# Image 1's first MLP product in two groups of fifteen on quarters

## The chip, the cores and the metric

The kernel runs on one core of a Trainium2 chip. The metric is the device time of one execution in microseconds, the median of several runs. A core has five engines with a queue of instructions each: PE multiplies matrices, DVE and ACT work element by element, POOL and SP issue most of the transfers. Each takes its instructions in the order written and waits at semaphores for the others.

## The reference

Eight images of 384 channels and 32 x 32 points, all in 32 bit, go through two layers.

```python
# layer 0, per image; tokens are the 1024 points
x1  = x + proj(attention(layernorm(x)))
h   = gelu(layernorm(x1) @ w_fc1.T + b_fc1)      # 384 -> 1536
y   = x1 + h @ w_fc2.T + b_fc2                   # 1536 -> 384
# layer 1, per image
z   = layernorm(depthwise_conv_7x7(y))
z   = gelu(z @ w1 + b1)                          # 384 -> 1536
z   = gamma * z * nx(z) + gbeta + z              # nx: a norm over the image
out = y + z @ w2 + b2                            # 1536 -> 384
```

## The kernel before

**Tiles.** Channels lie on the 128 partitions: an image is three tiles of 128 x 1024, the hidden layer twelve. Most work goes by halves of 512 points (`half`), and a matrix product of 128 x 128 by 128 x 512 is the unit; one such product is two passes in the trace.

**Products by thirds.** A 3 x 3 by 3 x 2 product of blocks takes 18 block products done directly. `tiles_by_thirds` (L458) does it in fifteen, in the order `SINGLY` (L94): each product takes a sum of weight blocks, made once and kept in DRAM, and a sum of data blocks, and `SUMS` says which results are added (DVE L483 and L486, ACT L480 and L488). The ten sums of data blocks are made on DVE, by `make_thirds` (L441) or, on 256 points, by `make_quarters` (L447, line L455).

**One round.** For image b the order of work is: qk by thirds, attention (L807), proj, fc1, fc2 (`by_thirds`, L1049, fifteen forms of four products, p0 to p14), and then for image b-1 the second layer: `grn_up` (h, w1) and `grn_down` (w2). The 7 x 7 convolution of image b-1 runs meanwhile, tap by tap on DVE (L1244: one multiply-add over an image's channel tile, 841 to 961 elements per partition), with some taps done by ACT and POOL (L1279, L1280). For image 0's convolution `start_conv` is called at L2115 and runs beside image 1's qk, attention and fc1. Images 2 to 7 find five taps of two channel tiles done already (`begin_convolution`); image 0's convolution has no such start.

**Who sets the order.** The program is written out by hand through `Flow` (L137). PE code calls `flow.pe(us)`, which moves a planned clock forward; chains (generators) that are due by that clock then write their next instructions, on DVE, ACT, POOL or SP, into the program. So a chain's `yield 1.5` is a planned distance and not a measured one, and once written the order on each engine is fixed. `flow.finish(chain)` writes the rest of a chain at once. While the list `hold` is not empty, `convolution` writes no tap (L1222) and `freely` (L1535) keeps the chains behind it back.

**fc1 (mlp, L1004).** For images 2 to 6 `fast_fc1` (L227) is true. Then the first half's tiles 6 to 11 are done by `gelu_group` (L952) in two groups of fifteen products on quarters: group 0 before tile 0, group 1 after tile 5; tiles 0 to 5 and the whole second half are direct (`gelu_half`, three products each, line L415). `hold` is set during group 0 and again from `rest()`, which is called after tile 1, to the end of group 1. `rest()` finishes attention's second half and does its proj (L760, L768). Then the second layernorm's second half is spawned (L551, L554, L561, L568, L572, L575, L594; its sums over channels on PE are L518, or L532 when the halves of the partitions are first folded by a POOL transfer, L526); with the groups its last three steps wait at the gate `ln2`. For images 0, 1 and 7 all twelve tiles are direct, `rest()` comes after tile 3, and nothing is held.

**The second layernorm's first half** runs under attention's second half, spawned in `attention` with `slow` and `wait`, which stretch its planned distances: 1.35 and 5.2 for image 1, 1.0 and 4.5 for the others but the last. For images with the groups, `make_quarters` follows in the same chain.

**What follows the second half's layernorm.** `conv_norm` (L1929) hangs two chains on it: `norm_of_next` (L1975), image 2's first layernorm, with the adds L2007 and L2009, POOL folds L1984 and L1991, and the PE sums L2001; and `end_soon` (L1971), which finishes the convolution, that is, writes all taps that are left in one go, then waits 22 planned us for image 1 (11 later on), and goes on with layernorm 3 of the convolution's result (again L551, L554, fold L526, PE sum L532, L561).

**Weights.** A ring of nine tiles is filled by SP in a fixed plan (L1888, `plan_fc1` L356). With the groups an image's fc1 takes twelve tiles, six of them sums from DRAM, in place of six.

Of the kernel before, what the change touches and what calls it, by code (L numbers as in the profile page):

```python
# [52 lines left out]
B, C, H, W = 8, 384, 32, 32  # L53
# [123 lines left out]
def block_kernel(  # L177
# [41 lines left out]
    exact = [False]  # L219
# [5 lines left out]
    s_fc1 = dram.tile([P, 2, len(FORMS), P], F32, tag="s_fc1", bufs=1, name="s_fc1")  # L225

    def fast_fc1(b):  # L227
        return not exact[0] and 1 < b < B - 1

    def half(h):  # L230
        return slice(h * NH, (h + 1) * NH)
# [16 lines left out]
    eps0 = const.tile([P, 1], F32, name="eps0")  # L248
# [558 lines left out]
    def attention(b, xt, qT, kT, last_tile, ready, first, next_image):  # L807


        sums = two.tile([P, 2 * NP * 8], F32, tag="sums", name=f"sums_{b}")  # L810
        outs, chains, ps, backs = {}, {}, {}, ({}, {})

        def scores(qh, m, t):
            s = ps_s.tile([P, 2, NH], F32, tag="s", name=f"s_{b}_{qh}_{m}_{t}")
            for j in range(2):
                for i in range(2):
                    k0 = t * P + 64 * i
                    nc.tensor.matmul(  # L818
                        out=s[64 * i : 64 * i + 64, j, :],
                        lhsT=kT[64 * j : 64 * j + HD, m, k0 : k0 + 64],  # L820
                        rhs=qT[64 * j : 64 * j + HD, m, half(qh)],
                        start=True,
                        stop=True,
                    )
            flow.pe(U)
            p = three.tile([P, 2, NH], F32, tag="p", name=f"p_{b}_{qh}_{m}_{t}")
            nc.scalar.activation(p, s, AF.Exp)  # L827
            return p

        def product(qh, m, t, p):  # L830
            if t == 0:
                for i in range(2):
                    outs[i] = o_tile(f"o_{b}_{qh}_{m}_{i}")
            for i in range(2):
                keys = slice(64 * i, 64 * i + 64)
                for j in range(2):
                    at = (2 * m + j) * VW
                    nc.tensor.matmul(  # L838
                        out=outs[i][64 * j : 64 * j + 64, :],
                        lhsT=v[keys, t, at : at + 64],  # L840
                        rhs=p[keys, j, :],
                        start=(t == 0),
                        stop=(t == KT - 1),
                    )
            flow.pe(U)
            if t == KT - 1:
                chains[qh, m] = flow.spawn(average(b, qh, m, dict(outs), sums, backs[qh]))

        steps = [(qh, m, t) for qh in range(2) for m in ORDER for t in range(KT)]
        ln_table()  # L850
        ln = None
        for n in range(len(steps) + 2):
            if n == 1:
                hold.clear()
                quiet.clear()
            if n == 2:
                last_tile()
            if n < len(steps):
                if steps[n][0] == 0 and steps[n][2] == 0:
                    ready(steps[n][1])  # L860
                ps[n] = scores(*steps[n])
            if n >= 2:
                product(*steps[n - 2], ps.pop(n - 2))
            if n - 2 in (len(steps) // 2 - 9, len(steps) - 9):
                quiet.append("averages")
            if n - 2 == len(steps) // 2 + 6:
                for chain in first:
                    flow.finish(chain)
                xn = one.tile([P, CT, N], F32, tag="xn", bufs=2, name=f"xn2_{b}")
                for m in (NP - 1, *range(CT)):  # L870
                    flow.finish(chains[0, m])
                proj(b, xt, 0)
                quiet.clear()
                next_image(b)
                slow = {1: 1.35, B - 1: 1.2}.get(b, 1.0)
                fold = "columns" if b else None
                ln = layernorm(xt, xn, 0, eps0, "g2", f"ln2_{b}", False, spaced=True, slow=slow, fold=fold, wait=5.2 if b == 1 else 4.5)
                if fast_fc1(b):
                    ln = sequence(ln, make_quarters(xn, hidden(b), 1.5))
                ln = flow.spawn(ln)  # L880

        def rest():
            for m in (NP - 1, *range(CT)):
                flow.finish(chains[1, m])
            for seen, op in ((low, ALU.min), (high, ALU.max)):
                ext = small.tile([P, 1], F32, tag="ext", name=f"ext_{b}_{op.name}")
                nc.vector.tensor_reduce(ext, sums, AX.X, op)
                nc.vector.tensor_tensor(seen, seen, ext, op)
            proj(b, xt, 1)
            quiet.clear()  # L890

        return ln, rest, xn
# [974 lines left out]
    def main():  # L1867
# [5 lines left out]
        xn = load_x(0, "xn", 4)  # L1873
# [13 lines left out]
        xt = load_x(0, "x", engine=nc.gpsimd)  # L1887
# [198 lines left out]
        for b in range(B):  # L2086
            if b == 0:
                folding = flow.spawn(after(None, folds(weights), 8))
                preparing = flow.spawn(after(None, prepare(weights, False), 4))
                singly = [flow.spawn(after(None, sums_for_tiles(i), 33 + 5 * i)) for i in range(2)]  # L2090
                aside = flow.spawn(after(folding, prepare(weights, True), 4))
            if b:
                flow.finish(state["thirds"])
            q_and_k = qk(b, state["xn"], weights if b else None)
            ln2, rest, xn = attention(b, xt, *q_and_k, (folding, aside) if b == 0 else (), next_image)
            if b == 0:
                for chain in singly:
                    flow.finish(chain)
                fc1_sums = flow.spawn(after(None, sums_for_fc1(), 22.0))
                shift = flow.spawn(after(None, prepare(weights, None), 4.0))  # L2100
            if b < B - 1:
                mlp(b, xt, xn, weights, b, ln2, rest, lambda: before_fc2(b), lambda ln: conv_norm(b, ln))
            else:
                acc = state["acc"]
                mlp_by_halves(b, xt, xn, weights, ln2, rest, last_convolution)
                fine = whether_fine()
            kept[b] = keep(b, xt)
            if b + 1 < B:
                acc = state["acc"]
            if b == 0:  # L2110
                xt = load_x(b + 1, "x")
                flow.finish(preparing)
                flow.finish(fc1_sums)
                flow.finish(shift)
                start_conv(b, 1.6, (9, 1.65), (10, 22.0), (60, 1.5))  # L2115
                next_values(1)
                continue
            if b < B - 1:
                xt = load_kept(b - 1, kept.pop(b - 1))
            flow.finish(state["norm3"])  # L2120
            if b < B - 1:
                flow.finish(state["w1"])
                y, gx = grn_up(b - 1, weights, b - 1, lambda: begin_conv(b))
                flow.finish(state["begin"])
                start_conv(b, 1.65 if b == B - 2 else 1.85, (23, 2.4), (24, 9.0), (25, 26.0), (72, 1.5))
                scale = flow.spawn(grn_scale(b - 1, gx, weights, b - 1, y))
                next_values(b + 1)
                flow.finish(scale)
                quiet.append("w2")
                grn_down(b - 1, y, xt, weights, b - 1, b - 1)  # L2130
                quiet.clear()
                xt = load_x(b + 1, "x")
            else:

                norm_b = flow.spawn(after(state["conv"], last_norm(LAST[1], 0.85)))
                norm_c = flow.spawn(after(norm_b, last_norm(LAST[2], 1.2)))
                y, gx = grn_up_straight(b - 1, acc, weights, b - 1)
                scale = flow.spawn(grn_scale(b - 1, gx, weights, b - 1))
                flow.finish(state["norm_a"])
                sums = small.tile([P, CT + 1, HT], F32, tag="gx_last", bufs=1, name="gx_last")  # L2140
                y_last = places(y)
                last_up(last[0], y_last, 0, sums, weights)
                flow.finish(scale)
                halves = lambda k, part: y[:, k, part]
                blocks = [(r, half(n)) for r in range(CT) for n in range(2)]
                args = b - 1, halves, kept[b - 1], weights
                grn_down_straight(*args, b - 1, b - 1, blocks[:-1])
# [157 lines left out]
```

## Time and profile before

| | us |
|---|---|
| median of three runs | 3212.09 |
| lowest and highest of them | 3211.55, 3214.67 |
| the profiled execution | 3213.02 |
| its span, first to last instruction | 3211.1 |
| PE's mean granted clock | 0.999 |

The stages of images 1 and 2 in the profiled execution, in us from the span's start, where the first instruction of each begins on PE:

| | image 1 | image 2 |
|---|---|---|
| attention, second half | 442.6 | 834.9 |
| fc1, first product | 484.9 | 877.3 |
| proj, second half | 495.3 | 889.2 |
| fc2, p0 | 558.5 | 949.0 |
| grn_up | 612.8 | 1002.6 |

In a view by time a row gives the start, the length, the engine, the line, the operation, what is written and read, the shape and the count; in brackets stands the time the engine was idle before it and what ended that. In a view by stretches a row gives the stretch and its length, then for PE, PE's weight loads, DVE, ACT and POOL the busy time and the number of instructions, then PE's granted clock, the share in which the transfer engines worked, and GB/s.

### The profile page before, as it was taken

Reading aid. Unit: us, or ns where it says so; the run is one execution under the profiler, and the core shown is the slowest. Engines: PE = TensorE matmul, PEld = TensorE weight load, DVE = VectorE, ACT = ScalarE, POOL = GpSimd, SP = SyncE. Lnnn points to the kernel's source line nnn. Section 1 sums busy time; section 2 is a strip of 40 time slices with the busy share of each in tenths; the row PEclk is TensorE's granted clock in tenths of the full one; section 3 lists DMA queues with packets and bytes.
Section 4 is the critical chain, followed back from the end, with each engine's and each line's share of the span. In section 5 each row is a group of like instructions: output and inputs, shape, how many; then the busy total and the mean of one; then the engine's idle time right before and its main releaser. Section 6 shows DMA issues by size and latency. Waiting matters only on the chain.

```text
span 3211.1 us, 39348 instructions
## 1 busy us (share of the span) xinstructions
PE 3196.2 (100%) x14204; PEld 1402.1 (44%) x14204; DVE 2550.4 (79%) x3587; ACT 1674.6 (52%) x2363; POOL 493.4 (15%) x592
## 2 busy tenths in 40 slices
PE   9999999999999999999999999999999999999999
PEld 5344434443444434444344443444435444344454
DVE  4547788897878978789787888888887788879964
ACT  3542763456644476444754637637365374732543
POOL 2102211112111121201112011120111201200000
PEclk9999999999999999999999999999999999999999
DMA  6435742647346564456546374463743638433244
GB/s 210 155 127 170 168 90 50 162 112 165 84 88 159 123 151 92 97 142 158 115 92 124 116 186 97 81 136 106 194 92 80 148 97 200 72 81 93 55 119 111
DMA packets 206052, 393.09 MB, mean 122 GB/s; under 512 B 42656, under 2 KB 48416, under 8 KB 205472
## 3 DMA queue, kind: packets, MB, share of 16 engines
q0 software_dynamic: 79296, 163.35, 26.6%
q1 hardware_dynamic: 126272, 226.49, 23.6%
q8 instruction: 114, 1.87, 0.2%
q10 hardware_dynamic: 288, 0.71, 0.1%
q14 instruction: 82, 0.67, 0.1%
HBM read 212.98 MB, written 40.11 MB: 79 GB/s over the span
## 4 chain that ended last, share of the span: by engine, by line
PE 97%; DVE 1%; DMA 1%; ACT 0%; issue 0%; SPq 0%; DVEq 0%; ACTq 0%
PE fc L415 15%; PE s L818 13%; PE o L838 13%; PE o_p L496 11%; PE fc_p L496 11%; PE v L738 4%; PE proj L760 4%; PE h_n L467 3%; PE h_z L467 3%; PE h_x L467 3%; PE h_last L1427 2%; PE o L1378 2%; PE h L402 2%; PE qk_n L467 2%; PE qk_z L467 2%; PE qk_x L467 1%
## 5 line engine op out<-in xcount | busy, mean ns | idle before, releaser
L1244 DVE SCALAR_TENSOR_TENSOR acc<-pad,vec,acc 128x870 f32<-128x870 f32 (+8 forms) x815 | 911.0, 1157 | 2.7
L827 ACT ACTIVATE p<-s 128x1024 f32<-128x1024 f32 x512 | 524.3, 1025 | 255.2 <-PE s L818 246.9
L818 PE MATMUL s<-qk 48*64 48x512 f32 x4096 | 538.7, 591 | 0.4 <-ACT qk L660 0.2
L838 PE MATMUL o<-p,v 64*64 64x512 f32 x4096 | 535.7, 589 | 0.0
L1280 POOL DMA_DIRECT2D acc<-tap x266 | 227.0, 859 | 1354.9 <-ACT tap L1279 647.5
L415 PE MATMUL fc<-xn,fc 128*128 128x512 f32 x972 | 427.7, 594 | 0.1
L496 PE MATMUL o_p<-y,w 128*128 128x512 f32 x664 | 289.0, 592 | 0.0
L838 PEld LDWEIGHTS o<-p,v 64*64 64x64 f32 x4096 | 166.4, 132 | 273.3 <-issue 265.0
L415 PEld LDWEIGHTS fc<-xn,fc 128*128 128x128 f32 x972 | 183.1, 190 | 229.2 <-issue 220.5
L818 PEld LDWEIGHTS s<-qk 48*64 48x64 f32 x4096 | 162.3, 132 | 275.9 <-issue 213.1
L496 PE MATMUL fc_p<-qk,fc 128*128 128x512 f32 x520 | 226.6, 593 | 0.3 <-DMA qk<-qk 0.3
L1279 ACT ACTIVATE tap<-pad,vec 128x512 f32<-128x512 f32 x266 | 195.1, 736 | 2.9 <-DMA acc<-tap 2.9
L496 PEld LDWEIGHTS o_p<-y,w 128*128 128x128 f32 x664 | 125.6, 190 | 157.7 <-issue 146.4
L1244 DVE SCALAR_TENSOR_TENSOR acc_last<-pad,vec,acc_last 128x377 f32<-128x377 f32 (+24 forms) x288 | 177.2, 688 | 0.6
L496 PEld LDWEIGHTS fc_p<-qk,fc 128*128 128x128 f32 x520 | 98.2, 190 | 126.9 <-issue 117.4
L508 ACT ACTIVATE qk<-fc,bfc_f 128x512 f32<-128x512 f32 x90 | 61.6, 685 | 160.4 <-PE fc L415 160.4
L508 ACT ACTIVATE hid<-fc,bfc_f 128x512 f32<-128x512 f32 x72 | 49.4, 687 | 158.3 <-PE fc L415 158.3
L779 DVE TENSOR_TENSOR attn<-o,attn 128x512 f32<-128x512 f32 x64 | 44.1, 689 | 109.9 <-ACT attn L777 108.8
L760 PE MATMUL proj<-attn,wproj_sb 128*128 128x512 f32 x288 | 127.5, 596 | 0.7 <-DVE attn L805 0.7
L738 PE MATMUL v<-wv_sb,xn 128*128 128x384 f32 x384 | 126.8, 487 | 0.0
L991 ACT COPY pad<-x 128x512 f32<-128x512 f32 x42 | 26.3, 634 | 187.7 <-DVE x L1083 187.7
L738 PEld LDWEIGHTS v<-wv_sb,xn 128*128 128x128 f32 x384 | 72.5, 190 | 50.1 <-issue 3.4
(446 smaller groups left out, 4594.7 us busy)
## 6 DMA issues: line engine op xcount, KB each, us to landing
acc<-tap POOLq DMA_DIRECT2D x266, 256.0 KB, 3.5
fc<-s_fc SPq DMA_DIRECT2D x91, 256.0 KB, 3.0
w<-s_w SPq DMA_DIRECT2D x91, 256.0 KB, 2.7
w<-s_w SPq DMA_DIRECT2D x72, 320.0 KB, 4.2
fc<-in_wfc SPq DMA_DIRECT2D x54, 384.0 KB, 4.0
y<-y POOLq DMA_DIRECT2D x38, 512.0 KB, 6.7
qk<-qk POOLq DMA_DIRECT2D x30, 512.0 KB, 9.4
qk<-s_qk SPq DMA_DIRECT2D x42, 320.0 KB, 4.9
```

The costliest lines, as they stand in the source:

```text
L415: nc.tensor.matmul(out=ps, lhsT=lhsT(k), rhs=rhs(k)[:, half(h)], start=(k == 0), stop=(k == nk - 1))
L467: nc.tensor.matmul(out=at, lhsT=weights.at(wname, g, slot // 5)[:, slot % 5, :], rhs=rhs[n], start=first, stop=True, skip_group_check=not ...
L496: nc.tensor.matmul(out=bank, lhsT=lhsT, rhs=rhs, start=k == 0, stop=k == len(pairs) - 1)
L508: nc.scalar.activation(dst, src, function, **kw)
L738: nc.tensor.matmul(out=ps[:, :C], lhsT=xn[:, k, t * P : (t + 1) * P], rhs=wv_sb[:, k, :], start=(k == 0), stop=(k == CT - 1),)
L760: nc.tensor.matmul(out=ps, lhsT=wproj_sb[:, m, ct * P : (ct + 1) * P], rhs=attn[:, m, :], start=(m == 0), stop=(m == CT - 1),)
L818: nc.tensor.matmul(out=s[64 * i : 64 * i + 64, j, :], lhsT=kT[64 * j : 64 * j + HD, m, k0 : k0 + 64], rhs=qT[64 * j : 64 * j + HD, m, half ...
L827: nc.scalar.activation(p, s, AF.Exp)
L838: nc.tensor.matmul(out=outs[i][64 * j : 64 * j + 64, :], lhsT=v[keys, t, at : at + 64], rhs=p[keys, j, :], start=(t == 0), stop=(t == KT - 1),
L1244: nc.vector.scalar_tensor_tensor(dst, window, tap, dst, ALU.mult, ALU.add)
L1279: nc.scalar.mul(t.rearrange("p (h w) -> p h w", w=W), window, tap)
L1280: nc.gpsimd.dma_start(out=acc[:, ct, half(h)], in_=t, accum_op=ALU.add)
```

## The change

`fast_fc1` becomes true for image 1, and with it everything that the code hangs on it: the two groups, the quarter sums, the twelve weight tiles, `rest()` after tile 1, the holds and the gate. The second layernorm's `slow` for image 1 goes from 1.35 to 1.0 and its `wait` from 5.2 to 4.5. The planned distance of taps 11 to 60 of image 0's convolution goes from 1.5 to 1.45.

```diff
     def fast_fc1(b):
-        return not exact[0] and 1 < b < B - 1
+        return not exact[0] and 0 < b < B - 1
...
-                slow = {1: 1.35, B - 1: 1.2}.get(b, 1.0)
+                slow = 1.2 if b == B - 1 else 1.0
                 fold = "columns" if b else None
-                ln = layernorm(xt, xn, 0, eps0, "g2", f"ln2_{b}", False, spaced=True, slow=slow, fold=fold, wait=5.2 if b == 1 else 4.5)
+                ln = layernorm(xt, xn, 0, eps0, "g2", f"ln2_{b}", False, spaced=True, slow=slow, fold=fold, wait=4.5)
                 if fast_fc1(b):
                     ln = sequence(ln, make_quarters(xn, hidden(b), 1.5))
...
-                start_conv(b, 1.6, (9, 1.65), (10, 22.0), (60, 1.5))
+                start_conv(b, 1.6, (9, 1.65), (10, 22.0), (60, 1.45))
```

## The prediction

> **What bounds the kernel now.** I read the page's busy and chain parts, then the stretch of image 1's MLP beside image 2's, then PE and DVE in order of time.
>
> ```profile
> PE 3196.2 (100%) x14204; PEld 1402.1 (44%) x14204; DVE 2550.4 (79%) x3587; ACT 1674.6 (52%) x2363; POOL 493.4 (15%) x592
> ...
> PE 97%; DVE 1%; DMA 1%; ACT 0%; issue 0%; SPq 0%; DVEq 0%; ACTq 0%
> ```
>
> PE is busy all the time and is 97% of the chain that ends last. So a product removed is worth its PE time, and a microsecond in which PE waits is lost for good. The stretches from fc1's first product to the next stage, image 1 and image 2:
>
> ```profile
> 484.90:612.80 127.90, 127.90 (x318) 55.63 (x315) 110.67 (x145) 43.19 (x65) 20.88 (x22) 1.00 0.42 90
> 877.30:1002.60 125.30, 125.30 (x344) 59.12 (x343) 97.05 (x146) 48.27 (x77) 24.18 (x26) 1.00 0.52 113
> ```
>
> Image 2, which has the groups, takes 2.6 us less. But DVE (third busy column) works 110.7 us of image 1's stretch and 97.1 of image 2's: image 1 carries the larger rest of a convolution. That is what has to be followed.
>
> **Products.** The change removes 18 products of 512 columns, which are 36 passes of 0.429 us start to start: 15.4 us. It adds two groups of 15 products of 256 columns. In image 2:
>
> ```profile
> 877.25 0.70 PE L467 MATMUL fc_n<-qk,fc1t 128*128 128x256 f32 x2
> ...
> 908.98 0.59 PE L467 MATMUL fc_n<-qk,fc1t 128*128 128x256 f32 x2
> ...
> 915.64 25.05 PE L415 MATMUL fc<-xn,fc 128*128 128x512 f32 x58
> ```
>
> The first group runs from 877.25 to 884.09 and the second from 908.98 to 915.64: 13.5 us. **-1.9 us** (at the median pass, 0.216 us, it would be -2.5). The 2.6 us between the stretches holds another 0.7, since image 2 also sums a variance on half the rows, so I use -1.9. The six added loads (3.5 us to landing in images 2 to 6) are issued during image 0's fc2 and qk of image 1, over 100 us ahead on SP; they cost nothing, and one landing if that cover failed. ACT gets some 5 us more to do (43.2 in image 1's stretch, 48.3 in image 2's, of 125): nothing, since it is idle more than half of the time.
>
> **Before the groups.** Ten quarter sums (0.34 us apart, 3.4 in all) go onto DVE between 437.6 and 485.6, where it waits today only 1.1, 2.0 and 0.4 us, each time for ACT's copy of an attention output. In the order in which the changed program issues its instructions one tap (1.1 us) fewer stands there. From L768 at 437.6 to the ninth sum the rows add up to 46.1 us of work, and two waits stay, 0.6 for a proj product and 1.8 for a copy: the ninth sum ends at 486.1. The group's fifth product needs it at 484.9 + 4 x 0.43 = 486.6. The last attention copy (L779) then runs 0.7 us late and the sixth product, which reuses a bank, waits 0.4 us; image 2 has some of such waits in its 6.8 us. **+0.2** (0 to 0.8). The ln2 wait shortened from 5.2 to 4.5 and slow from 1.35 to 1 only move planned places 3 us forward; ACT's rstd still ends before DVE asks. Between group 0 and L554 of the second half DVE then has one tap more than in image 2, 1.1 us, and image 2 ends L554 (899.9) only 0.5 before PE asks (900.4): **+0.6** (0 to 0.7) at the L518 sum.
>
> **The wait that the change makes.** While `hold` is set the convolution issues nothing (L1222), and the change sets it during group 0 and from rest() to the end of group 1. The twelve taps that run between 505 and 523 today and the four under group 0 are pushed behind group 1. Then end_soon empties the convolution at once, and layernorm 3's sums (L551, L554) stand behind it on DVE. Today:
>
> ```profile
> 525.62 18.09 DVE L1244 SCALAR_TENSOR_TENSOR acc<-pad,vec,acc 128x870 f32<-128x870 f32 x17
> 543.75 0.69 DVE L551 TENSOR_TENSOR ln_a<-acc 128x512 f32<-128x512 f32 x1
> ...
> 545.80 0.69 DVE L554 TENSOR_TENSOR attn<-attn,acc 128x512 f32<-128x512 f32 x1
> ```
>
> ```profile
> 516.17 35.35 PE L415 MATMUL fc<-xn,fc 128*128 128x512 f32 x82
> 551.45 0.71 PE L2001 MATMUL ln_sum<-ln,ones 32*128 32x256 f32 x8
> ...
> 557.46 0.65 PE L532 MATMUL ln_sum<-attn,ones 64*64 64x512 f32 x2
> ```
>
> Seventeen taps, sums done at 546.5, the POOL transfer that folds them issued at 546.8 and landed after 4.2; PE asks at 557.5, 6.5 us later. In the changed order 31 taps stand there in one row: the 17 and fourteen more. Sixteen are pushed there, and the closer plan of the first taps (50 x 0.05 = 2.5 planned us) takes two of them away again.
>
> Count from E, the start of fc1's second half. DVE: last L594 ends at E+1.4 (917.06 against 915.64), L2007 and L2009 2.4, seventeen taps 18.1, fourteen of 841 to 930 elements at 1.00 to 1.10 apart 14.8, L551 and L554 2.7: E+39.4; fold 0.3 + 4.2: E+43.9. PE: 36 products of 0.86, the L2001 sum 0.65, then four products of p0 and one of p1, 4.3, ahead of L532: E+35.9. PE waits **+8.0**. Bounds: the fold takes 2.3 to 5.2 in other places, so 6.1 to 9.0. PE is in order, so everything of fc2 is behind it. p5, which needs two DVE steps more, and POOL's fold_again, now behind two 512 KB transfers, come within 1 us of making PE wait again: 0 (to 1.0).
>
> **Clock.** After a wait, PE's clock:
>
> ```profile
> 157.00:160.40 3.40, 1.32 (x13) 0.20 (x5) 3.12 (x12) 1.02 (x1) 1.13 (x2) 1.00 0.17 72
> ...
> 162.00:165.40 3.40, 3.40 (x24) 0.84 (x16) 2.30 (x4) 2.44 (x4) 0.00 (x0) 0.51 0.79 325
> ```
>
> PE stood still 2.1 us, and soon after worked 3.4 us at a clock of 0.51: 3.4 x 0.49 = 1.7 us lost. A wait as long at 290.7 left the clock at 1.00. So 0 and 1.7 are both measured; 8 us is nearer to the one that paid: **+1.7** (0 to 3.3, two such stretches). The Trainium skill (TensorE: Matmul & The Clock Gate, What's actually happening) speaks against the change here: a whole idle window of about 3.4 us halves the clock until a busy window has passed. By it an 8 us wait always pays, an estimated 1.7 to 3.4 us; by the row at 290.7 alone it would pay nothing.
>
> **The tail.** Six L594 (4.0 us) and one L441 (0.6) run today before p6's sum:
>
> ```profile
> 579.77 2.07 DVE L594 SCALAR_TENSOR_TENSOR acc<-acc,vec,ln_rstd 128x512 f32<-128x512 f32 x3
> ...
> 585.62 0.69 DVE L1083 TENSOR_TENSOR fc_n<-fc_p,fc_n 128x512 f32<-128x512 f32 x1 [1.20 <-PE fc_p L496]
> ...
> 613.02 1.29 DVE L1083 TENSOR_TENSOR x<-fc_p,x 128x512 f32<-128x512 f32 x2 [2.22 <-PE fc_p L496]
> ```
>
> From 585.62 DVE has 25.2 us without a gap and then waits 2.2. In the changed order the seven stand behind p6's sum: 4.6 - 2.2 = 2.4 us late at the end of fc2. The first bank that grn_up reuses is freed at 616.66 and asked for at 612.8 + 5 x 0.86 = 617.1, so 0.4 is spare: **+1.9** (0 to 2.4).
>
> **Sum.** -1.9 + 0.2 + 0.6 + 8.0 + 1.7 + 1.9 = +10.5 us. The profiled execution took 3213.0 (span 3211.1 and 1.9 around it), so 3223.5; the median of the three runs shown is 0.9 lower, so **3222.6**.
>
> **Rivals.** *The queue is hidden* (not slower): all work on DVE ends before PE reaches L532, and only the products count, 3212.1 - 1.9 = 3210.2. It decides below 31 - 8.0/1.06, some 23 taps. For it: today 17 end 6.5 us early. Against: DVE has no wait in that row that it could fill, and a tap's time follows its size alone (the 870 element taps of this stretch mean 1116 ns, the 899 element ones 1145). *Quarters late*: DVE's three waits can't be used, since each is for an ACT copy, so the ten sums end up to 2.4 us later, group 0 waits and the proj behind it: 3225. For it: DVE is full in 437 to 485. Against: image 2 has the same ten sums in an equally full stretch. *No saving*: a 256-column pass at 0.257 us would eat the gain, 3224.5; the rows show 0.227 with their waits.
>
> **Numbers.** Forecast 0.74, of which 0.06 lies within 0.2%; quarters late 0.10; hidden 0.13, of which 0.02 is taken as faster; no saving 0.03, of which 0.01 is within. 0.2% is 6.4 us, about what a measurement of this kernel can tell from no change. Slower 0.80, same 0.18, faster 0.02. The forecast's terms at their low ends make -1.9 + 6.1 = +4.2 (3216) and at their high ends +15.3 (3227); one more for the late quarters gives 3216 to 3228. Hidden is left out.
>
> **What would show it.** Right: a row of 31 taps on DVE, ended near 561; a PE wait of about 8 us at L532 with the fold as its releaser; then a stretch at half clock. The two groups 13 to 14 us; DVE late by 2 us at p14. Wrong: L532 without a wait, or a wait before E, at the first group.

## The result and the profile after

The changed kernel takes 3222.35 us, the median of eight runs (3220.76 to 3225.19); the kernel before took 3212.19 beside it (eight runs, 3210.25 to 3214.67). The ratio is 1.0033, with a 95% interval from 1.0023 to 1.0042: slower by 10.2 us, and the forecast was 3222.6. The profiled execution of the changed kernel is the slowest of its eight, 3225.19, so what is added up below from its rows has to make 12.2 us against the 3213.02 of before's profiled one, and not 10.2.

The page's busy and chain parts, after:

```profile
PE 3200.7 (99%) x14228; PEld 1403.0 (44%) x14228; DVE 2563.0 (80%) x3619; ACT 1677.2 (52%) x2373; POOL 493.3 (15%) x592
...
PE 94%; DVE 3%; DMA 1%; issue 1%; ACT 0%; POOL 0%; SPq 0%; DVEq 0%; POOLq 0%; ACTq 0%
```

PE's share of the chain falls from 97 to 94% and DVE's rises from 1 to 3%: somewhere the end now hangs on DVE. The stretch from fc1's first product of image 1 to grn_up, as one row of the view by stretches:

```profile
484.54:624.06 139.52, 132.53 (x340) 61.84 (x339) 117.25 (x166) 45.86 (x73) 21.01 (x22) 0.96 0.44 97
```

It was 127.9 us and is 139.5, which is 11.6 more, and grn_up's first products take 1.9 more behind it. That is 13.5 and not 12.2, since before's execution lost 0.4 us more ahead of fc1, and 0.9 in image 6's attention at a wait that after's doesn't have. PE's busy time no longer equals the stretch, and its mean granted clock is 0.96: both a wait and a slower clock. DVE in order of time, from group 1 on (L483 is a sum of group 1):

```profile
522.14 0.42 DVE L483 TENSOR_TENSOR qk<-fc_n,qk 128x256 f32<-128x256 f32 x1 [0.38 <-PE fc_n L467]
...
524.79 0.74 DVE L594 SCALAR_TENSOR_TENSOR xn<-xn,vec,ln_rstd 128x512 f32<-128x512 f32 x1
...
527.86 32.85 DVE L1244 SCALAR_TENSOR_TENSOR acc<-pad,vec,acc 128x930 f32<-128x930 f32 x31
...
562.79 0.69 DVE L554 TENSOR_TENSOR attn<-attn,acc 128x512 f32<-128x512 f32 x1
563.40 3.87 DVE L2021 SCALAR_TENSOR_TENSOR xn<-ln_sum,xn 128x512 f32<-128x512 f32 x9
```

The 31 taps stand in one row, and the sums behind them end at 563.4. PE in the same time, and POOL's fold:

```profile
524.02 30.20 PE L415 MATMUL fc<-xn,fc 128*128 128x512 f32 x70
554.16 0.71 PE L2001 MATMUL ln_sum<-ln,ones 32*128 32x256 f32 x8
...
555.76 4.46 PE L496 MATMUL fc_p<-qk,fc 128*128 128x512 f32 x10
566.03 1.97 PE L532 MATMUL ln_sum<-ln_a,ones 64*64 64x512 f32 x4 [5.81 <-ACT qk L508]
```

```profile
562.72 0.85 POOL L526 DMA_DIRECT2D ln_a<-ln_a  x1 [19.93 <-DVE ln_a L554]
```

PE's last product ahead of L532 starts at 559.63 and the usual distance is 0.43, so PE asks at 560.06; it gets on at 566.03: 6.0 us. But the releaser in brackets is not the fold. The fold is issued at 562.72 and its transfer lands 2.7 us later (the view of the transfers), so at 565.4. ACT tells what came last:

```profile
552.55 0.69 ACT L508 ACTIVATE qk<-fc,bfc_f 128x512 f32<-128x512 f32 x1 [1.89 <-PE fc L415]
564.12 1.28 ACT L2023 ACTIVATE ln<-xn 128x512 f32<-128x512 f32 x2 [10.88 <-DVE xn L2021]
565.30 0.67 ACT L508 ACTIVATE qk<-fc,bfc_f 128x512 f32<-128x512 f32 x1
```

The L508 at 565.30 is the gelu of fc1's last tile. It ends at 565.97, and by the releaser in brackets it frees the bank that L532 takes. It stands on ACT behind the squares L2023 of image 2's layernorm, which wait for L2021 on DVE, which stands behind the taps. The source is the row of taps; the last leg runs through ACT and a bank, 0.6 us beyond the landing of the fold.

### The profile page after: what moved, and what is told of

Same layout as the page of the kernel before. It is cut to its first block, busy times and chain, and to the rows that moved or that the text cites. A ratio compares the mean times of both kernels' runs of the same rounds, so it can differ in the third digit from the quotient of the medians.

```text
span 3223.4 us, 39465 instructions
## 1 busy us (share of the span) xinstructions
PE 3200.7 (99%) x14228; PEld 1403.0 (44%) x14228; DVE 2563.0 (80%) x3619; ACT 1677.2 (52%) x2373; POOL 493.3 (15%) x592
## 4 chain that ended last, share of the span: by engine, by line
PE 94%; DVE 3%; DMA 1%; issue 1%; ACT 0%; POOL 0%; SPq 0%; DVEq 0%; POOLq 0%; ACTq 0%
PE s L818 13%; PE fc L415 13%; PE o L838 13%; PE o_p L496 11%; PE fc_p L496 9%; PE v L738 4%; PE proj L760 4%; PE h_n L467 3%; PE h_z L467 3%; PE h_x L467 3%; PE h_last L1427 2%; PE o L1378 2%; PE h L402 2%; PE qk_n L467 2%; PE qk_z L467 2%; PE qk_x L467 1%
## 5 line engine op out<-in xcount | busy, mean ns | idle before, releaser
L1244 DVE SCALAR_TENSOR_TENSOR acc<-pad,vec,acc 128x899 f32<-128x899 f32 (+8 forms) x815 | 911.9, 1159 | 2.7
L415 PE MATMUL fc<-xn,fc 128*128 128x512 f32 x936 | 412.4, 594 | 0.1
L496 PE MATMUL fc_p<-qk,fc 128*128 128x512 f32 x624 | 273.7, 596 | 0.5 <-DMA qk<-qk 0.4
L415 PEld LDWEIGHTS fc<-xn,fc 128*128 128x128 f32 x936 | 176.4, 190 | 219.3 <-issue 211.8
L496 PEld LDWEIGHTS fc_p<-qk,fc 128*128 128x128 f32 x624 | 118.5, 191 | 154.5 <-issue 143.1
L508 ACT ACTIVATE qk<-fc,bfc_f 128x512 f32<-128x512 f32 x108 | 73.9, 684 | 192.5 <-PE fc L415 192.5
L991 ACT COPY pad<-x 128x512 f32<-128x512 f32 x42 | 26.3, 635 | 192.3 <-DVE x L1083 192.3
L508 ACT ACTIVATE hid<-fc,bfc_f 128x512 f32<-128x512 f32 x48 | 32.9, 686 | 113.5 <-PE fc L415 113.5
```

The lines of the kernel that those rows point to most:

```text
L415: nc.tensor.matmul(out=ps, lhsT=lhsT(k), rhs=rhs(k)[:, half(h)], start=(k == 0), stop=(k == nk - 1))
L496: nc.tensor.matmul(out=bank, lhsT=lhsT, rhs=rhs, start=k == 0, stop=k == len(pairs) - 1)
L508: nc.scalar.activation(dst, src, function, **kw)
L1244: nc.vector.scalar_tensor_tensor(dst, window, tap, dst, ALU.mult, ALU.add)
```

## The experiments

Twelve more kernels were run. "Over" is against the kernel before in the same comparison (3211.8 to 3212.2). "Stretch" is the time from fc1 of image 1 to the end of grn_up's products in the profiled execution, over the 179.6 us of before. A wait is what the distance between the starts of two products has beyond the usual; "windows" are stretches of 3.4 us with a granted clock of about 0.5, from proj to grn_up. All in us. Group 0 is the first group of fifteen, p0 to p14 are fc2's forms, and h is grn_up's fourth product. "Over" is of medians and "stretch" of one execution, and what an execution loses outside the stretch isn't in it: against before's profiled execution, which lost 1.7 us of clock at 162 and 0.9 at the wait in image 6's attention, that is from 3.4 us less (taps4_out) to 5.2 and 6.5 more (more_help and plan100_l594, ahead of fc1).

| kernel | taps in the row | median | over | stretch | wait at L532 | other waits of PE from proj to grn_up | windows |
|---|---|---|---|---|---|---|---|
| changed | 31 | 3222.4 | 10.2 | 13.5 | 6.0 | group 0 0.8, L2001 0.8, h 1.9 | 3 |
| taps4_out | 27 | 3217.7 | 5.8 | 9.3 | 1.8 | group 0 0.8, L2001 1.1, h 1.9 | 2 |
| taps14_out | 17 | 3215.4 | 3.5 | 4.0 | 0 | group 0 0.8, p5 1.5, L2001 1.0, h 1.9 | 0 |
| before_held | 31 | 3216.0 | 4.2 | 5.9 | 0 | p5 0.6, L2001 1.6, h 1.9 | 0 |
| no_hold | 15 | 3225.0 | 13.1 | 11.3 | 0 | groups 4.0, L518 3.2, fc1 0.6, p5 1.5, L2001 0.5, h 1.9 | 0 |
| late_sums | 31 | 3224.4 | 12.5 | 12.4 | 0 | group 0 0.8, p2 0.6, p6 2.4, L2001 0.8, h 3.9 | 3 |
| stretched | 31 | 3226.2 | 14.4 | 14.7 | 6.0 | group 0 2.7, L2001 0.3, h 1.9 | 3 |
| taps14_early | 17 | 3220.4 | 8.5 | 10.8 | 3.1 | group 0 0.8, L2001 1.9 | 3 |
| more_help | 18 | 3231.5 | 19.7 | 10.8 | 3.1 | group 0 1.3, L518 0.8, group 1 0.4, L2001 2.5 | 2 |
| plan115 | 19 | 3215.6 | 3.6 | 4.1 | 0 | group 0 0.9, L518 1.2, p5 1.5, h 1.9 | 0 |
| plan115_l594 | 19 | 3213.5 | 1.4 | 2.8 | 0 | group 0 1.0, L518 1.0, p5 1.5, L2001 0.9 | 0 |
| plan100_l594 | 15 | 3219.1 | 7.0 | 2.2 | 0 | proj 4.0, group 0 1.4, L518 0.9, p5 1.5 | 1 |
| before_plan115 | 6 | 3211.1 | -1.0 | -0.2 | 0 | none | 0 |

The theory was the prediction's: the row of held taps makes PE wait at L532, and the late order behind it makes the tail. The rival: the groups themselves cost it, through their sums on DVE and their split products.

**taps14_out**: 14 taps of image 0's convolution left out, so that 17 stand in the row.

```diff
-        taps = [KS * KS - k for k in helped]
+        taps = [KS * KS - k - (o if us == 1.6 else 0) for k, o in zip(helped, (4, 5, 5))]
...
```

> The changed kernel with 14 taps of image 0's convolution left out (4, 5 and 5 of its three tiles; part of that convolution isn't computed), so that 17 taps instead of 31 stand in the row behind group 1; the order of everything else is that of the changed kernel. Theory of the held taps: layernorm 3's sums end some 15 us earlier, PE asks at L532 without a wait (6.0 us saved) and without the half clock behind it (3.0). The six L594 still stand behind p6's sum, so up to 2.2 us of the tail may stay, and with it the clock loss near 592 (1.8). Together 3211 to 3214. Rival, the groups themselves cost it (their sums on DVE, the split products): 3219 or more, since both groups are as they were.

Measured 3215.4, ratio 1.0011 (1.0002 to 1.0020). From proj to grn_up the wait at L532 and all half clock are gone, and h's 1.9 stays, as the theory said; the two groups are as they were, and all that is left of the loss is 3.5 us. It missed its range by 1.4. Waits that the theory did not count stand in the trace, 1.0 at L2001 and 1.5 at p5:

```profile
578.22 3.70 PE L496 MATMUL fc_p<-qk,fc 128*128 128x512 f32 x8 [1.31 <-DVE qk L1083]
```

The sums of p5's data (L1083) stand on DVE behind layernorm 3's steps in the changed order. In the changed kernel the 6 us wait ahead of it covers this one.

**taps4_out**: the same with 1, 1 and 2 taps left out.

> The changed kernel with 4 taps of image 0's convolution left out (1, 1 and 2 of its tiles, not computed): 27 taps in the row. Theory: the wait at L532 is what DVE's row is too long for the place of L532, so it shrinks by 4 x 1.07 = 4.3 us from 6.0 to 1.7, and as the short waits elsewhere (1.5 to 1.9 us) left the clock at full, the half clock goes too. What stays is what the kernel with 14 taps left out shows (3215.4): 3215.5 to 3218.5, 1.7 above that one. Rival, the clock falls behind any wait at L532: 3 us more, 3219 to 3221.

Measured 3217.7 (1.0019, 1.0010 to 1.0028), inside the range, and the wait at L532 is 1.8 for the expected 1.7 (its second sum comes another 0.5 late). From both kernels the row fits up to 31 - 5.97 / 1.07 = 25 taps or 27 - 1.82 / 1.07 = 25. The clock did not stay full, though: one window behind these 1.8 us and one behind 1.1 us at L2001.

**before_held**: the kernel before, with the holds alone.

```diff
         for m in range(HT // 2 if fast else HT):
...
-            waiting = gelu_half(hid, m, 0, xn, weights, wa, f"fc1_{b}", later=fast and m == HT // 2 - 1)
+            hold[:] = ["group"] * (m < 2) if b == 1 and m < 4 else hold; waiting = gelu_half(hid, m, 0, xn, weights, wa, f"fc1_{b}", later=fast and m == HT // 2 - 1)
...
-                rest()
+                rest(); hold.extend(["ln2"] * (b == 1))
...
-        flow.finish(ln)
+        hold.clear() if b == 1 else None; flow.finish(ln)
```

> The kernel before, without the groups, but with the convolution held where the change holds it (during the first two product groups of image 1's fc1, and from rest() to the end of the first half): 31 taps in a row behind fc1's first half, as in the changed kernel. Theory of the held taps: PE waits 6 to 8 us at L532 and loses some 3 us of clock behind it, and the tail comes too (2): 3222 to 3226, as slow as the changed kernel or slower, since it doesn't have the saved products. Rival, the groups cost it: 3212 to 3214, since there are none.

Measured 3216.0 (1.0017, 1.0008 to 1.0027): neither theory. The row has its 31 taps, the tail comes (1.9 at h), and yet L532 doesn't wait:

```profile
519.70 1.29 DVE L2007 TENSOR_TENSOR ln<-xn 128x512 f32<-128x512 f32 x2
520.90 1.29 DVE L2009 TENSOR_TENSOR ln<-ln,xn 128x512 f32<-128x512 f32 x2
522.11 32.81 DVE L1244 SCALAR_TENSOR_TENSOR acc<-pad,vec,acc 128x930 f32<-128x930 f32 x31
```

```profile
560.34 1.08 PE L532 MATMUL ln_sum<-ln_a,ones 64*64 64x512 f32 x4
```

PE asks at the same time as in the changed kernel, but the row starts at 522.11 and not at 527.86. Without groups nothing ahead of it on DVE waits for PE's last products. With them, the sums of group 1 and the L594 between them do, so the row can't start until group 1 is over. These 5.8 us are the groups' part of the 6.0 at L532, and the held taps only use up the room that was there: the row fits without the groups, though with nothing to spare (ACT's last L508 ends at 560.18 there), and the groups fit with 25 taps. The theory of the held taps alone fell here; what makes the wait is the long row **behind a barrier**.

**no_hold**: the changed kernel without the holds for image 1.

```diff
-                hold.append("group")
+                hold.extend(["group"][: b - 1])
...
-                    hold.append("ln2")
+                    hold.extend(["ln2"][: b - 1])
```

> The changed kernel, but image 1's groups don't hold the convolution back: its taps are issued between the sums, and 15 are left for the row behind group 1. Theory of the held taps: no wait at L532 and no half clock there, -9.0 us; against it, single taps of 1.1 us now stand ahead of the groups' sums, four in group 0 and four in group 1, which makes PE wait 1 to 4 us in the groups. 3213 to 3217. Rival, the groups themselves: what they cost stays and grows with the taps between, 3222 or more.

Measured 3225.0 (1.0041, 1.0028 to 1.0055; its profiled execution is its fastest, 3221.1). The time is on the rival's side; the theory had the place right and the price too low. L532 doesn't wait, but PE now waits 7.8 us before it. The waits of PE in this stretch, each with line, releaser, sum, count and longest:

```profile
PE ln_var L518 <- DVE ln_sq L575: 2.2, 1, 2.2
...
PE fc_n L467 <- DVE qk L483: 1.6, 3, 0.9
PE fc_x L467 <- DVE qk L483: 1.4, 1, 1.4
...
PE ln_sum L518 <- DVE ln_a L554: 0.7, 1, 0.7
```

A row of four taps (4.4 us) in the second layernorm is enough for L518 to wait. So the hold is no mistake: the taps have to go somewhere, and behind the groups is cheaper than among them.

**late_sums**: layernorm 3 planned later, so that PE asks at L532 9.5 us later.

```diff
-            yield 11.0 if b > 1 else 22.0
+            yield 11.0 if b > 1 else 31.0
```

> The changed kernel with layernorm 3's sums planned 9 us later behind the convolution (31 for 22), which puts L532 behind p3 on PE, eleven products of 0.86 us (9.5 us) later. The 31 taps stay in a row. Theory of the held taps: the wait at L532 (6.0) and its half clock (3.0) go, but the six L594 and the eight L441 now stand among p9 to p14 and DVE may be later at grn_up than it is (2.2): 3212 to 3217. Rival, DVE's work in total sets the end of fc2, not where L532 stands: the wait moves to grn_up, 3220 to 3224.

Measured 3224.4 (1.0037, 1.0023 to 1.0051), 0.4 above the rival's range: the rival has the mechanism right. The wait at L532 is gone, and PE waits 2.4 at p6 and 3.9 at h instead, with as much half clock (three windows). Behind the row DVE is late for everything that PE asks of it; which instruction shows it is only a matter of which comes first.

**stretched**: the changed kernel with the second layernorm drawn out again.

```diff
-                slow = 1.2 if b == B - 1 else 1.0
+                slow = {1: 1.35, B - 1: 1.2}.get(b, 1.0)
...
-                ln = layernorm(... wait=4.5)
+                ln = layernorm(... wait=5.2 if b == 1 else 4.5)
```

> The changed kernel with the second layernorm of image 1 drawn out again as in the kernel before (slow 1.35, wait 5.2); the groups and the 31 taps stay. Two more taps stand ahead of its L594 and two fewer among the ten sums. Theory (DVE is in order and the number of taps ahead of the ninth sum decides): group 0 waits the same 0.8 us or up to 1 us more; 3222 to 3224. Rival, the drawn out layernorm brings the quarters late by its 3 planned us: the groups wait 3 to 4 us, 3225 or more.

Measured 3226.2 (1.0048, 1.0034 to 1.0062), the rival's side. Group 0 waits for its quarters:

```profile
488.21 0.67 PE L467 MATMUL fc_z<-qk,fc1t 128*128 128x256 f32 x2 [1.60 <-DVE qk L455]
```

From its first product to the next one after it group 0 takes 11.0 us and not 7.8, with a window of half clock in it. So the two shortened distances are needed by the groups, and save 3 us of what they would cost.

**taps14_early**: 14 taps left out, and `yield 11.0 if b > 1 else 18.0` in `end_soon`, which puts the six L594 and one L441 ahead of p6's sum again.

> The kernel with 14 taps left out (3215.4), and layernorm 3 planned 4 us earlier behind the convolution (18 for 22): the six L594 and one L441 stand ahead of p6's sum on DVE again, as in the kernel before. Theory of the tail: DVE isn't late at p14, and the 1.9 us wait at h, which all variants with the L594 behind p6's sum show, goes; the 1.5 us at p5 may go or stay: 3212 to 3214. Rival, the wait at h comes from something else in image 1 (ACT's copies, the groups): 3215 to 3216.

Measured 3220.4 (1.0026, 1.0016 to 1.0037), outside both ranges. The wait at h is gone, as the theory of the tail said, but the edit did more: PE asks at L532 one product after p0's start, before the bank is free (0.9), and L561 now stands ahead of L2021, so that the second sum waits for the first one's reading:

```profile
556.55 1.08 PE L532 MATMUL ln_sum<-ln_a,ones 64*64 64x512 f32 x4 [0.78 <-ACT qk L508]
559.66 1.74 PE L532 MATMUL ln_sum<-attn,ones 64*64 64x512 f32 x4 [2.04 <-issue]
```

**more_help**: twelve more taps given to ACT and POOL (9, 11 and 11 for 5, 7 and 7; the expectation below says ten), and the same 18.0.

```diff
...
-... convolution(... helped=HELPED, ...)
+... convolution(... helped=HELPED if b else (9, 11, 11), ...)
...
-... help_convolution(acc, 2.5, taken) ...
+... help_convolution(acc, 2.5 if b else 1.8, taken, HELPED if b else (9, 11, 11)) ...
...
```

> The whole computation: the changed kernel with 10 more taps of image 0's convolution given to ACT and POOL (9, 11 and 11 of the three tiles for 5, 7 and 7, planned 1.8 us apart for 2.5), which leaves 18 taps in the row, and layernorm 3 planned 4 us earlier (18 for 22). Theory of the held taps and the tail: neither the wait at L532 nor that at h; what stays is group 0's 0.8 and up to 2.5 at p5 and L2001 against 1.9 us saved: 3211 to 3214. Rival, the added transfers on POOL or copies on ACT delay image 1's attention or the sums as much as the taps did: 3217 or more.

Measured 3231.5 (1.0065, 1.0052 to 1.0079), on the rival's side. It carries the fault of taps14_early (its 3.1 at L532 is the same), and the help isn't free: PE waits 2.8 us in qk for ACT's L488, behind the added copies, and attention's first half, from its first product to proj, takes 73.4 us for 71.1 in the changed kernel. DVE also waits 2.0 us ahead of the row for a transfer of the helped taps, and the 18 taps take 21.6 us, 1.2 each where the changed kernel's take 1.06.

**plan115**: the first taps planned closer, so that twelve more stand ahead of the row, nine of them ahead of proj's first half.

```diff
-                start_conv(b, 1.6, (9, 1.65), (10, 22.0), (60, 1.45))
+                start_conv(b, 1.6, (9, 1.65), (10, 22.0), (60, 1.15))
```

> The whole computation: the changed kernel with the first taps of image 0's convolution planned 1.15 us apart instead of 1.45. Twelve more taps then stand ahead of the second attention half, where DVE waited 11 us in all for ACT's copies, and 19 instead of 31 stand in the row. Theory of the row: as with 14 taps left out (3215.4), no wait at L532 and no half clock there; the waits in group 0 (0.8), at p5 (1.5), L2001 (1.0) and h (1.9) stay: 3214 to 3217. Rival, DVE has no real room in attention: the copies' followers (L779, L805) come late and PE waits in attention or in group 0: 3219 or more.

Measured 3215.6 (1.0012, 1.0003 to 1.0021), as expected: with the whole computation it is 3.6 us over the kernel before, where the changed kernel is 10.2 over, and as fast as with 14 taps left out.

**plan115_l594**: plan115, and only the seven instructions moved.

```diff
-                how = dict(wait=5.6, late=3.5 if b > 1 else 0, fold_squares=b > 1) ...
+                how = dict(wait=5.6, late=3.5 if b > 1 else -2.4, fold_squares=b > 1) ...
```

> The kernel before it in this list, and the last step of layernorm 3 planned 2.4 us earlier (late = -2.4 for image 0's), which puts the six L594 and one L441 ahead of p6's sum on DVE; PE's order isn't touched. Theory of the tail: the 1.9 us wait at h goes and nothing else moves, so 1.9 us below the one before it: 3212 to 3215. Rival, the seven instructions aren't what DVE is late by: the same time as the one before it within 0.5 us.

Measured 3213.5 (1.0006, 0.9997 to 1.0015), 2.1 below plan115; the interval holds 1, so the 1.4 us over the kernel before isn't shown to be a loss. DVE by time:

```profile
583.39 2.08 DVE L594 SCALAR_TENSOR_TENSOR acc<-acc,vec,ln_rstd 128x512 f32<-128x512 f32 x3 [3.01 <-ACT ln_rstd L589]
585.38 2.07 DVE L594 SCALAR_TENSOR_TENSOR acc<-acc,vec,attn 128x512 f32<-128x512 f32 x3
587.37 0.69 DVE L441 TENSOR_TENSOR thirds<-acc 128x512 f32<-128x512 f32 x1
587.97 0.69 DVE L1083 TENSOR_TENSOR fc_n<-fc_p,fc_n 128x512 f32<-128x512 f32 x1
```

They run while DVE would wait for p6 (6.4 us in plan115), and grn_up has no wait left. The tail is shown by itself: seven instructions in another place, 1.9 us. In the profiled execution 4.4 us of waits stay, against 1.9 saved.

**plan100_l594**: the same with 1.0 for 1.15.

> As the one before it, with 1.0 us for 1.15: 15 taps in the row, four fewer. Theory of the row: below some 25 taps the row is hidden and nothing more is won, 3212 to 3215, the same within 1 us. If shorter rows still help, DVE is late after the row as well, at p5 and L2001: 1 to 2 us less. Rival, attention has no more room: 2 us more or worse.

Measured 3219.1 (1.0024, 1.0015 to 1.0033): the rival. A shorter row wins nothing, and attention's first half is full:

```profile
442.74 4.11 PE L760 MATMUL proj<-attn,wproj_sb 128*128 128x512 f32 x6 [3.83 <-DVE attn L805]
```

**before_plan115**: the control, the kernel before with 1.15 for 1.5.

> A control: the kernel before, with the taps planned 1.15 apart instead of 1.5 and nothing else; 6 taps instead of 17 behind fc1's first half. All theories: the row is hidden in both, so it stays at 3212 within 1 us; if attention has no room for the taps it is slower by what the first kernel of this list loses there.

Measured 3211.1 (0.9997, 0.9988 to 1.0006), with no wait of PE in image 1's MLP. Room on DVE alone is worth nothing there; no version with the groups came below the kernel before.

## Why the prediction was right, step by step

The time was right to 0.3 us of the median. The mechanism was right up to the last leg of the wait, and several terms were off in size and balanced. By the rows of the profiled execution:

| term | predicted | measured | |
|---|---|---|---|
| products | -1.9 | -1.8 | the groups took 7.8 and 6.7, of which 0.8 is waits |
| group 0's waits | +0.2 | +0.8 | at its bound, 0.51 and 0.29; a wait there was also its sign of being wrong |
| L518's sum | +0.6 | 0 | DVE was in time; in plan115, with one tap more ahead of it, L518 waits 1.2 |
| wait at L532 | +8.0 | +6.0 | just under its range of 6.1 to 9.0 |
| p5 and L2001 | 0 | +2.0 | L2001 waits 0.8, and its sums, one by one, take 1.2 longer; above the 1.0 allowed |
| clock | +1.7 | +4.6 | three windows, less the part of the first that PE waited through; above the 3.3 allowed |
| tail | +1.9 | +1.9 | at grn_up's fourth product, through ACT's copies (L991) of DVE's late sums |
| sum | +10.5 | +13.5 | as the stretch has it; less 1.3 outside it, +12.2 |

The wait at L532: the prediction had DVE's sums end at E+39.4, which is 563.4, and they end at 563.4; it had PE ask at E+35.9, and PE asks at 560.06, E+36.0. The step that failed is "fold 0.3 + 4.2". The fold landed in 2.7 here, and it wasn't the last: the bank was, freed by an L508 on ACT at 566.0, and the prediction has no such term. That before_held doesn't wait shows that fourteen more taps alone are harmless there; the prediction's sum had the barrier in it ("last L594 ends at E+1.4") without naming it as half of the cause. Its rival "hidden below some 23 taps" was near: 25.

The clock: "8 us is nearer to the one that paid" took one window for a wait that lost two. It had two waits of 2.1 us to go by, of which one paid; the length alone doesn't decide (last section). The profile by stretches, granted clock third from the end:

```profile
564.80:568.20 3.40, 2.17 (x8) 0.59 (x8) 2.63 (x8) 2.91 (x5) 0.00 (x0) 0.54 0.28 43
568.20:571.60 3.40, 3.40 (x5) 1.17 (x4) 3.40 (x6) 0.00 (x0) 0.00 (x0) 0.50 0.00 0
...
592.10:595.50 3.40, 3.40 (x5) 1.51 (x6) 0.00 (x0) 1.98 (x4) 0.00 (x0) 0.54 1.09 202
```

and the third, at 592, stands behind the wait at L2001 that the prediction had put at nothing. That wait it named, POOL's fold_again behind two 512 KB transfers, with 1.0 at most: it is 2.0 with the sums that now come one by one (590.16 to 591.97, and 577.74 to 578.38 before), and 1.7 of clock go with it.

"Quarters late" did not come in the changed kernel, and came in stretched, without the two shortened distances, where group 0 took 3.2 us longer against the rival's 2.4.

So the forecast met the median by luck, with errors of opposite sign: the wait at L532 2.0 too long, the clock, group 0 and L2001 together 5.5 too short, L518 0.6 too long. The median lies 2.8 us under the profiled execution, which fits one or two windows of half clock fewer in most runs. The other seven have no profile, but the record has their mean granted clock: 0.998 or 0.999 against 0.997 in the profiled one, and 0.001 of 3223 us is 3.2 us, about two windows. The slower three of the seven are those at 0.998.

## What to carry to other kernels

When work is pushed behind a group on an in-order engine, ask two things of the row that results: how long it is, and what ahead of it waits for another engine, since that sets when it may start; here a row of 31 instructions didn't make PE wait at L532 without the barrier, and with it cost 6 us of wait and 3 of clock. Then follow the row's lateness through every queue that reads from it, not only the transfer that the code shows next: the bank that PE waited for was held by an unrelated instruction on ACT, behind one that waited for the row. Moving the asking instruction later doesn't help when the serving engine is late for all that follows; moving work into that engine's own waits does, up to where they are full.

## What the runs showed of the hardware

The same wait upstream of the change cost clock in one execution and none in another. It stands near 292, in fc2 of image 0: 2.1 us idle in brackets, 2.3 from start to start beyond the usual. Before:

```profile
292.98 3.31 PE L496 MATMUL fc_p<-fc_e,fc 128*128 128x512 f32 x7 [2.12 <-issue]
```

```profile
292.00:295.40 3.40, 2.42 (x6) 1.10 (x7) 3.40 (x5) 0.00 (x0) 1.07 (x2) 1.00 0.43 148
```

After:

```profile
290.89 5.37 PE L496 MATMUL fc_p<-fc_e,fc 128*128 128x512 f32 x8 [2.12 <-issue]
```

```profile
292.00:295.40 3.40, 3.40 (x5) 1.32 (x5) 2.86 (x3) 0.00 (x0) 0.69 (x2) 0.50 0.41 154
162.00:165.40 3.40, 3.40 (x36) 1.21 (x30) 2.56 (x4) 3.05 (x6) 0.63 (x2) 1.00 0.75 312
```

Before had its half clock at 162 (0.51) and after has it at 292. The half clock comes in stretches of 3.41 us, one or two at a time, and they lie on a grid. Stretches of 0.05 us put their beginnings in the changed kernel's trace at 292.0, 565.1 and 592.4: the distances, 273.1 and 27.3 us, are 80 and 8 times 3.413. In taps4_out (562.8 and 586.7), late_sums (291.6, 585.2, 626.1), stretched (292.1, 490.1, 568.6) and more_help (291.5, 356.4, 571.4, 598.7) the distances are whole multiples of it too. Where the grid lies differs from one execution to the next; in a trace without half clock among its products it is read from the one that begins behind the last product.

What decides is how much of a wait lies between two neighbouring points of the grid. The wait near 292 has the same 2.3 us in all fourteen traces. In the changed kernel it goes from 288.60 to 290.89, all but 0.01 of it between the points 288.61 and 292.03; in before it goes from 290.69 to 292.98, and the point 291.74 cuts it. In five traces (changed, late_sums, stretched, more_help, plan115) at least 2.1 us of it lie between two points, and the next 3.4 us run at half clock in all five; in the other nine at most 1.8 do, and none of them does. The 1.9 at h lies whole between two points in six kernels and was followed by no half clock; the waits in group 0 of stretched, 2.4 us between 486.7 and 490.1, were. The 4.0 at proj in plan100_l594 is cut into two parts of 2.0, and half clock followed the second part alone, so the limit lies near there for full 128 x 128 products. So 1.7 us per stretch come and go from run to run with the place of the grid.

Where narrow sums on 64 or 32 rows stand in the same stretch, less was enough: a wait of 0.8 at L2001 in the changed kernel and of 1.1 in taps4_out, with sums that then come one by one over 1.8 us. These sums may count as little work; no run took them away, so this stays open.

The Trainium skill (TensorE: Matmul & The Clock Gate, What's actually happening) says that a whole idle window of about 3.4 us halves the clock and that the windows run free of the kernel. The grid agrees; half clock behind stretches in which PE waited 2.1 to 2.4 of 3.41 us doesn't fit a whole idle window, and the measurement decides here.
